# A fused attention and mixture-of-experts kernel: the block lists finished before the second sequence's norm, their constant rows made in the first stage, and the second group of table rows queued behind the first masked scores

## The chip, the cores and the metric

The kernel runs on one core of a Trainium2 chip. The metric is the device time of one execution in microseconds (us). Several executions are timed and their median is given; one further execution is recorded by the profiler. The engines are named as in the profile: PE (matrix multiply), PEld (its weight loads), DVE (vector), ACT (scalar), POOL (GpSimd) and SP (the queue that issues most DMAs). "L586" is line 586 of the kernel.

## The reference

The input x has 8 sequences of 512 tokens of 512 floats. Each token is layer-normed to xn. Two branches use xn:

```
q, k, v = xn@Wq, xn@Wk, xn@Wv              # 16 heads of 32; silu and rotation on q, k
o       = decayed causal linear attention, in chunks of 128 tokens, state carried
s       = (rmsnorm per head of (o * sigmoid(xn@Wg1@Wg2)) * norm_weight) @ Wo
p       = softmax(xn @ gate_w.T);  top 4 of 16 experts, weights renormalised
mixed   = sum over the 4 experts of weight * (silu(xn@Wg[e]) * (xn@Wu[e])) @ Wd[e]
g       = silu(mixed + shared expert * sigmoid(xn @ shared_gate_w))
out     = x + s * g
```

## The kernel before, in words

All arithmetic on PE is in 32-bit floats. The work goes through four stages.

**First stage** (until about 214 us). `first()` norms and transposes each sequence, routes its tokens, and computes the shared expert; sequence 0's attention (`sequence(0, ...)`) is woven in. `sort()` (L375) then ranks all 16,384 token-expert choices: for each choice its row in the list of blocks, `posi` (L459), split into a position and a block number in `sp` (L465). Everything of this stage lies in a pool `p1` on the right side of the on-chip memory, which is closed at L1056.

**Second stage** (about 214 to 301 us). The pool `exps` takes the same memory; its tile `wexp` will hold all 16 experts' weights. Eleven are loaded at once (L1063). The space of the last five (`LATE`) first holds scratch for `table()` (L483), which inverts `posi` into `slot`, the list of the token in each row of each block of 128 rows. For each of 8 groups of 16 choice lists, `make` (L520) writes two tables of zeros and ones on DVE, called `place` and `block`, by comparing `sp` with a row of counts (`count`, an iota at L512); `number` (L538) scales half of `place` by token numbers on ACT; 16 small matmuls `pn` (L566) multiply them, and DVE adds the result into `acc` (L575). The last step multiplies `acc` by `fold` (`pslot`, L582) and writes `slot` (L586). Two homes in `wexp` are used in turn, so group n+2 waits for the `pn` of group n. `table()` is a generator with 33 steps after its first; sequence 1's attention (L1071) calls one step after each of its large matmuls in `product` and `value` (`between[0]`, L618 and L662). Twenty-eight steps are taken in the loop over head groups, four in `value(2, 3)`, and the last one after the sequence (L1072). Steps 30, 31 and 32 are, for the last group, the issue of three expert loads, the 16 matmuls and the addition.

After its loop over the four head groups `sequence(1, ...)` ends with the branch at L869: the gate projection of sequence 2 (`gate_1`), the squares of the norm (`squares`, L777), the reciprocal of the root (`inverse`), the last value product of sequence 2, and `normed` (L794), which broadcasts the scales through PE into the four `a` banks of PSUM and multiplies on DVE (L806).

**Third stage** (about 301 to 706 us). The 136 blocks of 128 gathered tokens are run through their experts: 112 in pairs, then single blocks. For each pair: `gather` (L1110, an indirect DMA issued by POOL), `turn_rows` (L1117, a DMA that transposes, issued by SP), `transpose_x` (L1122, PE), `join` (L1132, copies by ACT: L1138 from PSUM and L1142 from the transposed rows), `prepare` (L1155, DVE copies of one expert's weights, with a run-time offset into `wexp`, and of the row weights), `gate_up` (L1167, PE), and `down` (L1207, PE, again with a run-time offset into `wexp`). Before that come three gathers, `experts_of_blocks` (L1250: six dependent DVE operations giving each block's expert), the four output projections of sequence 1 (`project`, L809, whose results `spill` copies on ACT and stores), and `begin` (L1218), which also does the second half of sequence 2's gate (`gate_2`). The last two experts are loaded from ACT's DMA queue (L1077).

**Fourth stage** (about 706 us to the end): sequences 2 to 7's attention, the gathers of each token's four expert results and the output.

Order of work: the framework derives all waits from the tiles read and written, and it orders each engine's queue by its own schedule. The kernel overrides that order in places. `on_pe()` chains most matmuls of the attention in the order in which they are traced. `behind(engine)` (L216) and `tc.issue_after(ins)` put an instruction behind another one in the same engine's queue, without a wait for its end. Tiles with one `tag` share `bufs` places. With `reuse_waits="tile"` the tiles of a pool wait for the tiles that held the memory before.

The lines that set the order around the change:

```python
        if n == FIRST:
            gate_1(n)
            squares(b)
            inverse(b)
            value(n, 3)
            normed(b)
            return
...
    sequence(1, lambda: None, spill)
    for _ in filling:
        pass
...
    for j in range(3):
        gather(j)
    experts_of_blocks()
    for t in range(NC):
        spill(FIRST - 1, t, project(FIRST - 1, t))
```

Of the kernel before, what the change touches and what calls it, by code (L numbers as in the profile page):

```python
# [19 lines left out]
P = 128  # L20
# [17 lines left out]
TMP = 4  # L38
# [59 lines left out]
def tile_block(ctx: ExitStack, tc: tile.TileContext, a: dict, out: bass.AP):  # L98
# [93 lines left out]
    posi = p1.tile([P, TOPK, NT], I32, tag="posi", name="posi")  # L192

    sp = const.tile([P, 2, TOPK * NT], F16, tag="slot", name="sp")

    eoff = const.tile([P, 2, NBQ], I32, tag="eoff", name="eoff")
# [286 lines left out]
    def table(room):  # L483
# [16 lines left out]
        count = part(2 * NB, QUAD)  # L500
# [7 lines left out]
        half_token, fold, acc = flat(NT), flat(HALF), flat(2 * NB)  # L508
        nc.scalar.copy(half_token, token)
        for h in range(0, P, HALF):  # L510
            nc.scalar.copy(fold[h : h + HALF], ident[h : h + HALF, h : h + HALF])
        nc.gpsimd.iota(  # L512
            count, [[1, 2 * NB], [0, QUAD]], base=0, channel_multiplier=0,
            allow_small_or_imprecise_dtypes=True)
# [5 lines left out]
        def make(i):  # L520
            place, block = homes[i // GROUP % 2]
            for u in range(0, quads, quads // 2):
# [6 lines left out]
                nc.vector.tensor_tensor(  # L529
                    place[:, us], counts(HALF), rows(sp[:, 0, lists], HALF), ALU.is_equal)  # L530
                if u == 0:
# [3 lines left out]
                nc.vector.tensor_tensor(  # L535
                    block[:, us], counts(2 * NB), rows(sp[:, 1, lists], 2 * NB), ALU.is_equal)
# [49 lines left out]
        nc.vector.tensor_scalar(t, pt[:, :NB], float(B * N // 2), None, ALU.add)  # L586
# [113 lines left out]

    def scores(b, g):
# [44 lines left out]
        for j in range(HG):  # L746
            s = scr[0].tile([P, NC, C], F32, tag="sc", name=f"sc_{b}_{g}_{j}", bufs=4)
            nc.vector.tensor_tensor(  # L748
                s, pss[j].rearrange("p (c t) -> p c t", t=C),
                dmask[:, g * HG + j].unsqueeze(1).to_broadcast([P, NC, C]), ALU.mult)  # L750
            sc_of[g].append(s)
# [41 lines left out]

    def normed(b):  # L794
# [9 lines left out]
        for c in range(NC):  # L804
            oc = on_of[b][:, :, c * C : (c + 1) * C]
            nc.vector.tensor_tensor(  # L806
                oc, oc, pbs[c].rearrange("p (g t) -> p g t", t=C), ALU.mult)
# [10 lines left out]
    def enter(b, step=lambda: None, ps=None):  # L818
# [9 lines left out]
        step()  # L828

    def sequence(b, step, projected, before=None, defer=False, also=lambda: None):  # L830
# [197 lines left out]
    halves(0)  # L1028
    xs_of.pop(0)
# [58 lines left out]
    homes = [blkp.tile([P, ROW], U16, tag=f"xg{j}", name=f"xg{j}") for j in range(HOMES // 2)]  # L1088
    homes += [more[:, j * ROW : (j + 1) * ROW] for j in range(HOMES // 2)]
# [11 lines left out]
    by_dve = [0]  # L1101

# [7 lines left out]
    def gather(j, its):  # L1110
        for i in its:
            nc.gpsimd.indirect_dma_start(  # L1112
                out=row(i), out_offset=None, in_=xn_d,
                in_offset=bass.IndirectOffsetOnAxis(ap=slot[:, i : i + 1], axis=0))
# [17 lines left out]
    def join(j, its):  # L1132
# [8 lines left out]
        for u in range(n):  # L1141
            (nc.vector.tensor_copy if j in by_dve else nc.scalar.copy)(  # L1142
                xt[:, u, KP:, :].bitcast(U16).rearrange("p k (t h) -> p h k t", h=2),
                pls[j % 2][:, u].rearrange("p (h k) t -> p h k t", h=2))
# [99 lines left out]
    def aside(j):  # L1244
        if j == PAIRS:
# [4 lines left out]
    def experts_of_blocks():  # L1250
        half = NBQ * 2 * E
        room = xts.rearrange("p j u k t -> p (j u k t)")
        cm = room[:, :half].rearrange("p (b e) -> p b e", e=2 * E)
        ef = room[:, half : half + NBQ]
        ei = room[:, half + NBQ : half + 2 * NBQ].bitcast(I32)
        nc.vector.tensor_tensor(
# [206 lines left out]
```

## Time and profile before

| | |
|---|---|
| median of 3 runs | 1152.28 us (1148.9 to 1152.95) |
| the profiled execution | 1155.04 us |
| its span, from the first to the last instruction | 1153.2 us |
| busy in the span: PE, DVE, ACT, POOL | 1117.9, 736.7, 429.3, 446.8 us |
| mean granted TensorE clock | 0.99 |
| instructions | 21330 |

How to read it: the profile lists instructions by engine and time, and ahead of an instruction the idle time of its engine with what ended it. A matmul's share of "busy" is not a share of its peak. The span is what the instructions cover; the profiled execution took 1.84 us more than that. The waits of PE before 330 us are listed in the answer on PE's waits; the stretch from 225 to 330 us is the one that the change touches, and outside it PE is busy almost throughout.

### The profile page before, as it was taken

The page shows a single profiled execution, that of the slowest core. Times are in us where ns is not written, and L with a number is a line of the kernel's source. Part 1 is how long each engine was busy: PE and PEld are TensorE (multiplying, and loading weights), DVE is VectorE, ACT ScalarE, POOL GpSimd, SP SyncE. Part 2 cuts the span into 40 slices and gives each one's busy share as a digit, 9 for nine tenths or more (in the row PEclk, how much of TensorE's full clock was granted, in tenths as well). Part 3 has the DMA queues.
Part 4 walks back from the last instruction along what each step waited for, and adds up shares of the span by engine and source line. Part 5 has one row for each costly group of instructions (what it writes and reads, how often), then busy time and mean ns, then how long its engine had stood idle before and what let it go on. Part 6 is the DMA issues. An engine that isn't in the chain of part 4 may idle for free. (4 is left out here: it accounts for less than half of the span.)

```text
span 1153.2 us, 21330 instructions
## 1 busy us (share of the span) xinstructions
PE 1117.9 (97%) x7670; PEld 679.7 (59%) x7670; DVE 736.7 (64%) x1580; ACT 429.3 (37%) x927; POOL 446.8 (39%) x427
## 2 busy tenths in 40 slices
PE   7999999989899999999999999999999999999998
PEld 4445554445477777777777775555645545545554
DVE  6358734899334444555444445968879597697784
ACT  3223424154253333333333342353351522522541
POOL 3213100300233333333333322764877857958211
PEclk9999999989999999999999999999999999999999
DMA  9975431191799999999999994833737637434012
GB/s 338 319 276 194 156 127 47 51 352 40 217 200 236 220 244 238 238 241 237 253 233 234 272 215 178 323 101 108 254 116 230 183 108 244 150 122 145 29 36 75
DMA packets 163931, 218.49 MB, mean 189 GB/s; under 512 B 89840, under 2 KB 99184, under 8 KB 161776
## 3 DMA queue, kind: packets, MB, share of 16 engines
q1 hardware_dynamic: 142416, 145.18, 40.5%
q0 software_dynamic: 21120, 70.34, 23.9%
q10 hardware_dynamic: 288, 1.57, 0.4%
q8 instruction: 63, 1.03, 0.4%
q14 instruction: 44, 0.36, 0.1%
HBM read 126.78 MB, written 72.43 MB: 173 GB/s over the span
## 5 line engine op out<-in xcount | busy, mean ns | idle before, releaser
L1180 PE MATMUL pgu<-xts,wst 128*128 128x256 f32 x896 | 204.3, 381 | 0.0
L1180 PEld LDWEIGHTS pgu<-xts,wst 128*128 128x128 f32 x896 | 171.3, 191 | 46.7 <-issue 13.4
L1112 POOL DMA_INDIRECT xg<-xn_d,slot x69 | 65.7, 953 | 229.4 <-DVE w L1163 118.4
L1313 POOL DMA_INDIRECT yg<-y_d,place x128 | 142.5, 1113 | 31.1 <-issue 18.5
L1215 DVE TENSOR_SCALAR y<-py,w 128x512 f32<-128x512 f32 x136 | 101.6, 750 | 44.7 <-PE py L1211 31.0
L1211 PE MATMUL py<-wexp,slb 128*128 x272 | 129.9, 593 | 0.0
L615 PE MATMUL pv<-wv,xT 128*128 128x512 f32 x256 | 120.1, 610 | 3.1 <-DMA xT<-xT_d 2.0
L659 PE MATMUL pq<-xT,wq 128*128 128x512 f32 x256 | 118.2, 604 | 0.3 <-PEq L1278 0.3
L659 PE MATMUL pk<-xT,wk 128*128 128x512 f32 x256 | 118.2, 603 | 0.0
L1192 ACT ACTIVATE slb<-pgu 128x256 f32<-128x256 f32 (+1 forms) x80 | 28.1, 351 | 222.5 <-PE pgu L1180 184.1
L813 PE MATMUL pw<-wo,on 128*128 128x512 f32 x224 | 103.9, 612 | 5.8 <-DVE m L1351 5.8
L1193 DVE TENSOR_TENSOR slb<-slb,pgu 128x256 f32<-128x256 f32 (+1 forms) x80 | 30.5, 381 | 119.5 <-ACT slb L1192 118.1
L1112 POOL DMA_INDIRECT more<-xn_d,slot x67 | 63.5, 948 | 93.1 <-DVE w L1163 56.9
L1355 POOL TENSOR_TENSOR xo<-xo,m 128x512 f32<-128x512 f32 x31 | 45.3, 1460 | 131.2 <-DVE m L1351 123.3
L1142 ACT COPY xts<-pl 128x512 uint16<-128x512 uint16 x110 | 84.1, 767 | 9.0 <-DMA pl<-xg 9.0
L659 PEld LDWEIGHTS pq<-xT,wq 128*128 128x128 f32 x256 | 48.1, 193 | 55.3 <-issue 53.9
L748 DVE TENSOR_TENSOR sc<-ps,dmask 128x512 f32<-128x512 f32 x128 | 79.0, 676 | 0.9 <-PE ps L723 0.9
L615 PEld LDWEIGHTS pv<-wv,xT 128*128 128x128 f32 x256 | 46.3, 191 | 53.7 <-issue 47.1
L813 PEld LDWEIGHTS pw<-wo,on 128*128 128x128 f32 x224 | 42.5, 196 | 57.1 <-issue 47.7
L659 PEld LDWEIGHTS pk<-xT,wk 128*128 128x128 f32 x256 | 46.2, 189 | 50.7 <-issue 48.3
L1161 DVE COPY wst<-wexp 128x512 f32 x112 | 42.8, 424 | 39.8 <-DVE y L1215 18.7
L1211 PEld LDWEIGHTS py<-wexp,slb 128*128 128x128 f32 x272 | 45.5, 191 | 27.4 <-issue 26.8
(196 smaller groups left out, 1716.5 us busy)
## 6 DMA issues: line engine op xcount, KB each, us to landing
y_d<-y SPq DMA_DIRECT2D x136, 256.0 KB
wexp<-in_experts SPq DMA_DIRECT2D x14, 768.0 KB
sh_d<-sh SPq DMA_DIRECT2D x32, 256.0 KB
xT<-xT_d SPq DMA_DIRECT2D x8, 1024.0 KB
m<-sh_d SPq DMA_DIRECT2D x32, 256.0 KB
xo<-in_x SPq DMA_DIRECT2D x32, 256.0 KB
out<-xo SPq DMA_DIRECT2D x31, 256.0 KB
x<-in_x SPq DMA_DIRECT2D x7, 1024.0 KB
```

Source lines behind the costliest of these rows:

```text
L615: nc.tensor.matmul(pv, lhsT=xT_of[b][:, k, t * P : (t + 1) * P], rhs=wv[:, k, :], start=(k == 0), stop=(k == KC - 1))
L659: nc.tensor.matmul(ps, lhsT=w[:, k, g * P : (g + 1) * P], rhs=xT_of[b][:, k, :], start=(k == 0), stop=(k == KC - 1))
L748: nc.vector.tensor_tensor(s, pss[j].rearrange("p (c t) -> p c t", t=C), dmask[:, g * HG + j].unsqueeze(1).to_broadcast([P, NC, C]), ALU.mult)
L813: nc.tensor.matmul(pw, lhsT=on_of[b][:, g, t * P : (t + 1) * P], rhs=wo[:, g, :], start=(g == 0), stop=(g == G - 1))
L1112: nc.gpsimd.indirect_dma_start(out=row(i), out_offset=None, in_=xn_d, in_offset=bass.IndirectOffsetOnAxis(ap=slot[:, i : i + 1], axis=0))
L1142: (nc.vector.tensor_copy if j in by_dve else nc.scalar.copy)(xt[:, u, KP:, :].bitcast(U16).rearrange("p k (t h) -> p h k t", h=2), pls[j % ...
L1161: nc.vector.tensor_copy(to, wflat[:, bass.ds(off + u * KC * F, KC * F)])
L1180: nc.tensor.matmul(pg[:, o * 2 * P : (o + 1) * 2 * P], lhsT=wst[j % 2][k // KP][:, (k % KP * 2 + o) * F :][:, :F], rhs=xt[:, :, k, :], sta ...
L1211: nc.tensor.matmul(py, lhsT=hT[:, u * P : (u + 1) * P], rhs=wflat[:, bass.ds(off + KC * 2 * F, D)], start=True, stop=True)
L1215: gone.append(nc.vector.tensor_scalar(y, py, w[:, u : u + 1], None, ALU.mult).ins)
L1313: nc.gpsimd.indirect_dma_start(out=yg, out_offset=None, in_=y_d, in_offset=bass.IndirectOffsetOnAxis(ap=place[:, r, g : g + 1], axis=0))
L1355: nc.gpsimd.tensor_tensor(xo, xo, m, ALU.add)
```

## The change

- `TMP`, the number of places for the tag `tmp` (rotated keys and queries, spilled projections, block results), goes from 4 to 5.
- `count`, `half_token` and `fold` move out of the scratch in `wexp` into tiles of their own, and are made on POOL in the first stage, behind `halves(0)`. `posi` moves from the pool `p1` to `const`.
- In `make`, the two comparisons of the first half of group 1 are queued behind the last masked score of DVE so far (L748).
- In sequence 1, the last five steps of `table()` come right after the loop over head groups: four of them, `gate_1`, and the fifth. `experts_of_blocks` follows `inverse`, with its scratch now in `wexp`, each operation queued behind the last.
- The loads of the last two experts move from ACT's queue, before the blocks, to SP's queue in the block loop at j = 1 and j = 3.
- The block rows' homes swap: the first three gathers now write to the memory of sequence 1's values. Gathers, row transposes, the copies L1142 and the first run-time offsets are tied to the order in which they are traced.

```diff
-TMP = 4
+TMP = 5
...
-    posi = p1.tile([P, TOPK, NT], I32, tag="posi", name="posi")
+    posi = const.tile([P, TOPK, NT], I32, tag="posi", name="posi")
+    count = const.tile([P, 2 * NB, QUAD], F16, tag="count", name="count")
+    half_token = const.tile([P, NT], F16, tag="half_token", name="half_token")
+    fold = const.tile([P, HALF], F16, tag="fold", name="fold")
...
-        count = part(2 * NB, QUAD)
...
-        half_token, fold, acc = flat(NT), flat(HALF), flat(2 * NB)
-        nc.scalar.copy(half_token, token)
-        for h in range(0, P, HALF):
-            nc.scalar.copy(fold[h : h + HALF], ident[h : h + HALF, h : h + HALF])
-        nc.gpsimd.iota(
-            count, [[1, 2 * NB], [0, QUAD]], base=0, channel_multiplier=0,
-            allow_small_or_imprecise_dtypes=True)
+        acc = flat(2 * NB)
...
-                nc.vector.tensor_tensor(
-                    place[:, us], counts(HALF), rows(sp[:, 0, lists], HALF), ALU.is_equal)
+                with tc.issue_after(masked[0]) if i == GROUP and u == 0 else nullcontext():
+                    nc.vector.tensor_tensor(
+                        place[:, us], counts(HALF), rows(sp[:, 0, lists], HALF), ALU.is_equal)
+                with tc.issue_after(masked[0]) if i == GROUP and u == 0 else nullcontext():
+                    nc.vector.tensor_tensor(
+                        block[:, us], counts(2 * NB), rows(sp[:, 1, lists], 2 * NB),
+                        ALU.is_equal)
...
-        nc.vector.tensor_scalar(t, pt[:, :NB], float(B * N // 2), None, ALU.add)
+        with behind(DVE):
+            nc.vector.tensor_scalar(t, pt[:, :NB], float(B * N // 2), None, ALU.add)
...
-            nc.vector.tensor_tensor(
+            masked[:] = [nc.vector.tensor_tensor(
                 s, pss[j].rearrange("p (c t) -> p c t", t=C),
-                dmask[:, g * HG + j].unsqueeze(1).to_broadcast([P, NC, C]), ALU.mult)
+                dmask[:, g * HG + j].unsqueeze(1).to_broadcast([P, NC, C]), ALU.mult).ins]
...
-            nc.vector.tensor_tensor(
-                oc, oc, pbs[c].rearrange("p (g t) -> p g t", t=C), ALU.mult)
+            scaled[:] = [nc.vector.tensor_tensor(
+                oc, oc, pbs[c].rearrange("p (g t) -> p g t", t=C), ALU.mult).ins]
...
+    def experts_of_blocks():
+        half = NBQ * 2 * E
+        room = wflat[:, (E - LATE // 2) * WE :]
...
+        with behind(DVE):
+            nc.vector.tensor_reduce(ef, cm, axis=AX.X, op=ALU.add)
...
         if n == FIRST:
+            for _ in range(4):
+                next(filling)
             gate_1(n)
+            next(filling, None)
             squares(b)
             inverse(b)
+            experts_of_blocks()
             value(n, 3)
             normed(b)
             return
...
     halves(0)
+    with behind(POOL):
+        nc.gpsimd.tensor_copy(half_token, token)
+    for h in range(0, P, HALF):
+        with behind(POOL):
+            nc.gpsimd.tensor_copy(fold[h : h + HALF], ident[h : h + HALF, h : h + HALF])
+    with behind(POOL):
+        nc.gpsimd.iota(
+            count, [[1, 2 * NB], [0, QUAD]], base=0, channel_multiplier=0,
+            allow_small_or_imprecise_dtypes=True)
...
-    for _ in filling:
-        pass
     between[0] = lambda: None
     slot = slots[0]
-    for e in range(E - LATE // 2, E):
-        nc.scalar.dma_start(wexp[:, e, :], a["experts"][:, e, :])
     left.close()
...
-    homes = [blkp.tile([P, ROW], U16, tag=f"xg{j}", name=f"xg{j}") for j in range(HOMES // 2)]
-    homes += [more[:, j * ROW : (j + 1) * ROW] for j in range(HOMES // 2)]
+    homes = [more[:, j * ROW : (j + 1) * ROW] for j in range(HOMES // 2)]
+    homes += [blkp.tile([P, ROW], U16, tag=f"xg{j}", name=f"xg{j}") for j in range(HOMES // 2)]
...
         for u, i in enumerate(its):
-            nc.sync.dma_start_transpose(pls[j % 2][:, u], row(i)[:, D : 2 * D])
+            with tc.issue_after(turned[-1]) if turned else nullcontext():
+                turned.append(nc.sync.dma_start_transpose(
+                    pls[j % 2][:, u], row(i)[:, D : 2 * D]).ins)
...
-            (nc.vector.tensor_copy if j in by_dve else nc.scalar.copy)(
-                xt[:, u, KP:, :].bitcast(U16).rearrange("p k (t h) -> p h k t", h=2),
-                pls[j % 2][:, u].rearrange("p (h k) t -> p h k t", h=2))
+            with behind(DVE if j in by_dve else ACT):
+                (nc.vector.tensor_copy if j in by_dve else nc.scalar.copy)(
+                    xt[:, u, KP:, :].bitcast(U16).rearrange("p k (t h) -> p h k t", h=2),
+                    pls[j % 2][:, u].rearrange("p (h k) t -> p h k t", h=2))
...
     def aside(j):
+        if j in (1, 3):
+            e = E - LATE // 2 + j // 2
+            nc.sync.dma_start(wexp[:, e, :], a["experts"][:, e, :])
         if j == PAIRS:
             load_xT(FIRST)
...
     for j in range(3):
         gather(j)
-    experts_of_blocks()
     for t in range(NC):
         spill(FIRST - 1, t, project(FIRST - 1, t))
     on_of.pop(FIRST - 1)
+    gone += scaled
     begin(0, lambda: gate_2(FIRST, banks="aakd"))
```

The gathers (L1112) are also put `behind(POOL)`, and `turned` is cleared in the branch for more than 136 blocks.

More of the change, by code (lines that the diff above doesn't have):

```diff
@@ L534, in make @@
                             :, : GROUP // 2], HALF), ALU.mult)
-                nc.vector.tensor_tensor(
-                    block[:, us], counts(2 * NB), rows(sp[:, 1, lists], 2 * NB), ALU.is_equal)
         def number(i, some):
@@ L699, in by_token @@
         kd_of[g] = pk[:, (NC - 1) * P :], kd
+    masked = []
     def scores(b, g):
@@ L792, in inverse @@
         nc.vector.reciprocal(rs_of[b], rs_of[b])
+    scaled = []
     def normed(b):
@@ L805, in normed @@
             oc = on_of[b][:, :, c * C : (c + 1) * C]
-            nc.vector.tensor_tensor(
-                oc, oc, pbs[c].rearrange("p (g t) -> p g t", t=C), ALU.mult)
+            scaled[:] = [nc.vector.tensor_tensor(
+                oc, oc, pbs[c].rearrange("p (g t) -> p g t", t=C), ALU.mult).ins]
     def project(b, t):
@@ L828, in enter @@
         step()
+    def experts_of_blocks():
+        half = NBQ * 2 * E
+        room = wflat[:, (E - LATE // 2) * WE :]
+        cm = room[:, :half].rearrange("p (b e) -> p b e", e=2 * E)
+        ef = room[:, half : half + NBQ]
+        ei = room[:, half + NBQ : half + 2 * NBQ].bitcast(I32)
+        with behind(DVE):
+            nc.vector.tensor_tensor(
+                cm, end.rearrange("p w e -> p (w e)").unsqueeze(1).to_broadcast([P, NBQ, 2 * E]),
+                iota_b.unsqueeze(2).to_broadcast([P, NBQ, 2 * E]), ALU.is_le)
+        with behind(DVE):
+            nc.vector.tensor_reduce(ef, cm, axis=AX.X, op=ALU.add)
+        with behind(DVE):
+            nc.vector.tensor_copy(ei, ef)
+        with behind(DVE):
+            nc.vector.tensor_scalar(ei, ei, E - 1, None, ALU.bitwise_and)
+        with behind(DVE):
+            nc.vector.tensor_scalar(eoff[:, 0], ei, float(WE), None, ALU.mult)
+        with behind(DVE):
+            nc.vector.tensor_scalar(eoff[:, 1], ei, float(D), None, ALU.add)
     def sequence(b, step, projected, before=None, defer=False, also=lambda: None):
@@ L1101, in tile_block @@
     by_dve = [0]
+    turned = []
     def inside(f):
@@ L1111, in gather @@
         for i in its:
-            nc.gpsimd.indirect_dma_start(
-                out=row(i), out_offset=None, in_=xn_d,
-                in_offset=bass.IndirectOffsetOnAxis(ap=slot[:, i : i + 1], axis=0))
+            with behind(POOL):
+                nc.gpsimd.indirect_dma_start(
+                    out=row(i), out_offset=None, in_=xn_d,
+                    in_offset=bass.IndirectOffsetOnAxis(ap=slot[:, i : i + 1], axis=0))
     @inside
@@ L1248, in tile_block @@
     kept.clear()
[L1250 to L1256, printed above, removed]
-            cm, end.rearrange("p w e -> p (w e)").unsqueeze(1).to_broadcast([P, NBQ, 2 * E]),
-            iota_b.unsqueeze(2).to_broadcast([P, NBQ, 2 * E]), ALU.is_le)
-        nc.vector.tensor_reduce(ef, cm, axis=AX.X, op=ALU.add)
-        nc.vector.tensor_copy(ei, ef)
-        nc.vector.tensor_scalar(ei, ei, E - 1, None, ALU.bitwise_and)
-        nc.vector.tensor_scalar(eoff[:, 0], ei, float(WE), None, ALU.mult)
-        nc.vector.tensor_scalar(eoff[:, 1], ei, float(D), None, ALU.add)
     for j in range(3):
         gather(j)
-    experts_of_blocks()
     for t in range(NC):
@@ L1281, in tile_block @@
         gone.clear()
+        turned.clear()
         for j in range(3):
```

## The prediction

> **What bounds the kernel now.** I read the page first (PE is busy 97% of the span), then PE's waits, then the timelines of PE, DVE, ACT and POOL from 225 to 330 us. After 330 us PE is busy without a break until the blocks end, so only the transition into the blocks can give time. PE's idle time there, with the rows after it:
>
> ```profile
> 237.35 0.90 PE L691 MATMUL pk<-ident,kT 128*128 128x128 f32 x3 [4.16 <-DVE state L738]
> 238.04 5.19 PE L659 MATMUL pq<-xT,wq 128*128 128x512 f32 x6
> ...
> 255.87 2.74 PE L659 MATMUL pq<-xT,wq 128*128 128x512 f32 x6
> ...
> 265.92 4.54 PE L615 MATMUL pv<-wv,xT 128*128 128x512 f32 x6 [2.02 <-DMA xT<-xT_d]
> ...
> 300.83 0.26 PE L582 MATMUL pslot<-wexp 128*64 128x143 f16 x2 [2.76 <-DVE on L806]
> 301.01 15.67 PE L813 MATMUL pw<-wo,on 128*128 128x512 f32 x32
> ...
> 319.88 1.15 PE L645 MATMUL p<-g,wg 32*128 32x128 f32 x26 [1.90 <-ACT so L996]
> 320.97 5.41 PE L1180 MATMUL pgu<-xts,wst 128*128 128x256 f32 x16
> 326.21 0.60 PE L1126 MATMUL pt<-ident,more 128*128 128x128 f32 x4
> 326.65 3.62 PE L1180 MATMUL pgu<-xts,wst 128*128 128x256 f32 x16
> ```
>
> The reader sees four idle times, and that what follows each runs slowly: six matmuls of pq took 5.19 us after the first and 2.74 us undisturbed; 16 of pgu took 5.41 and then 3.62. The granted clock in the 5 us after them is 0.61 to 0.69, elsewhere 1.00. So each idle time is paid almost twice. DVE in the same stretch:
>
> ```profile
> 224.77 0.29 DVE L465 CAST sp<-bl 128x256 f16<-128x256 int32 x1
> 229.48 0.43 DVE L529 TENSOR_TENSOR wexp<-wexp,sp 128x512 f16<-128x512 f16 x1 [4.42 <-POOL wexp L512]
> ...
> 236.54 0.18 DVE L736 COPY state<-pk 128x32 f32<-128x32 f32 x1
> ...
> 297.00 1.36 DVE L1256 TENSOR_TENSOR xts<-end,iota_b 128x1152 f32<-128x1152 f32 x1 [0.60 <-PE pv L615]
> ...
> 300.09 2.47 DVE L806 TENSOR_TENSOR on<-on,pb 128x512 f32<-128x512 f32 x4
> 302.48 0.30 DVE L586 TENSOR_SCALAR slot<-pslot 128x143 int32<-128x143 f32 x1
> ...
> 305.13 0.76 DVE L1161 COPY wst<-wexp 128x512 f32 x2 [2.17 <-DMA wexp<-in_experts]
> ```
>
> `sp` is ready at 225.06, but the tables start only at 229.48: DVE waits for POOL's iota, and POOL waited for the store of posi, which holds the memory of `wexp`. Then two groups of tables (7.1 us) stand ahead of the state copies at 236.54, for which PE's transposes wait. Later L1256 and its five followers stand ahead of L806, and `slot` comes last.
>
> ```profile
> 226.21 3.24 POOL L512 IOTA wexp<- 128x572 f16 x1 [9.01 <-DMA at_d<-posi]
> ...
> 303.68 1.23 POOL L1112 DMA_INDIRECT xg<-xn_d,slot  x1 [71.49 <-DVE eoff L1263]
> ```
>
> ```profile
> 318.01 1.38 ACT L1142 COPY xts<-pl 128x512 uint16<-128x512 uint16 x2 [7.53 <-DMA pl<-xg]
> 319.26 1.05 ACT L996 COPY so<-pw 128x512 f32<-128x512 f32 x2
> ```
>
> The gather starts at 303.68; its transposed rows reach ACT at 318.01. ACT stands in wait for them with two spill copies queued behind, and those hold the PSUM bank for which PE waits at 317.99. That chain (slot, gather, transposed rows, spill, gate, first pgu) sets when the blocks begin.
>
> **Part A, 225 to 289 us: −6.5 us.** The iota and the copies leave the path, and posi no longer holds `wexp`, so the first tables can start at 225.06: 4.42 us earlier. DVE is nearly full: from 229.48 to 288.15 it is busy 55.68 of 58.67 us, so it can gain at most 4.42 + 2.99 = 7.4 us. The second group is put behind the masked scores, whose matmuls end at 229.5, so the state copies run at about 229.3 instead of 236.54 and the transposes need not wait. PE then saves 4.16 us idle, 5.19 − 2.74 = 2.45 of slow pq, and 0.90 − 0.49 = 0.41 of slow transposes (0.49 is the next such group): 7.0 us. The 2.02 us before pv stays: that load of xT is issued when the last pq has read the old xT, so it moves along with PE. What becomes late next is DVE, at 4.4 to 7.4 us. I take 6.5, nearer to PE's 7.0 since both bounds lie close; the range keeps 4.4 to 7.4.
>
> **Part B, 289 us to the end of the first pgu: −7.3 us.** The last `pn` and `pslot` go ahead of the squares, so `slot` needs: output ends at 289.13, pn 1.2 us, the addition 0.45, fold 0.26, L586 0.30: about 292 against 302.8 us. Gather and transposed rows took 303.68 to 318.01 = 14.3 us; from 293 they end at about 308 (310 if the three expert loads issued at 287.4 slow them), before the projections end at about 312. So ACT no longer stands in front of the spill copies, and the 1.90 us goes, with the slow pgu, 5.41 − 3.62 = 1.79. The six expert operations (3.4 us by 297.00 to 300.1 and 302.7 to 302.95, less the slot between them) now start after the reciprocal, which in this alignment ends at about 294.3, so they end at 297.8; the broadcast on PE ends at about 297.4, and the first L806 then takes 0.6. PE waits about 1.1 instead of 2.76 us. An idle time of 1.04 us earlier in this trace left the clock at full, so I also count the slow projections away: 15.67 − 14.00 (the same 32 matmuls at 214.12) = 1.67. With the 0.25 before the last square: 1.66 + 0.25 + 1.67 + 1.90 + 1.79 = 7.3 us. If the rows came late after all, 3.7 of it would be lost.
>
> A rule may be weighed here. The Trainium skill, "TensorE: Matmul & The Clock Gate", section "HAM oscillation — how this bites in real kernels", says that idle times above some 3.4 us are what throttles the array. This trace disagrees: 1.90, 2.02 and 2.76 us were each followed by slow matmuls, though 1.91 us at 1025.87 was not. By the rule the 1.67 and 1.79 would not be gained, and the total would be 3.5 us less.
>
> **Part C, the two late expert loads: +3 us.** DVE's L1161 and PE's L1211 read `wexp` at run-time offsets. The row at 305.13 shows that the very first such read waits for the last expert's load, so a read waits for all loads traced before it. At j = 1 the load is issued after the weight copies of pair 2, which end about 0.7 us after the first pgu; the first `down` follows that pgu by 4.3 us (326.21 to 330.54). The load of one expert took 301.12 to 305.13 = 4.0 us at a DMA share of 0.75; in the blocks the share is about 1.0. So PE would stand 0.4 us if it lands in 4.0, and 4.4 us in 8. At j = 3 the copies leave 5.3 us by the same spacing: 0 to 2.7 us. A slow clock adds up to 1.7 each. The schedule may also put the next pgu in front, and then nothing is lost. Bounds 0 and 10 us; I take 3, nearest to landing in 5 to 6 us.
>
> **What costs nothing.** The three copies and the iota in the first stage take at most 3 × 0.71 (a POOL copy of 128x512) + 3.24 = 5.4 us and fit into POOL's idle time before 25.03:
>
> ```profile
> 16.34 2.85 POOL L268 COPY hs<-x 128x512 uint16<-128x512 uint16 x4
> 25.03 0.24 POOL L251 TENSOR_SCALAR rstd<-mv 128x4 f32<-128x4 f32 x1 [5.83 <-DVE mx L328]
> ```
>
> Without that cover rstd would be late, but DVE has 4.94 us idle at 34.69 behind it. A rule speaks against this move: the Trainium skill, "GPSIMD Engine Reference", section "Key points", says that POOL shares its SBUF interfaces with DVE and contends with two-input DVE work. No row shows the iota beside DVE work. By the rule DVE could lose up to the iota's length there, and the idle time just named would still take it.
>
> The fifth `tmp` place, the order of gathers, row transposes and L1142 change no duration. In the blocks PE is never idle, so they can cost only if they hold PE up; ACT needs about 2.5 of each 5.6 us per pair. In the last stage the fifth place can shift DVE's order; the idle times there (1.16, 2.61, 1.91) bound that at about 2 us either way, and I take 0. SP loses nothing: today it waits 5.6 us for spill copies behind ACT's L543 at 232, and that goes with the earlier tables.
>
> **Sum.** −6.5 − 7.3 + 3 = −10.8 us. Against the profiled execution (1155.04, span 1153.2, so 1.84 around it) that is 1144.2. That execution lies 2.76 us above the median of the runs, so against the median 1152.28 I forecast 1141.5 us.
>
> **Rivals.**
> 1. *DVE becomes the bound of part A.* It is already 95% busy there; if the moved group only pushes other table work in front of PE, A gives 2 to 4 us instead of 6.5: 1144 to 1146, say 1145.5. For: tables, rotations and masks fill DVE from 244 to 285. Against: its own chain starts 4.42 us earlier. Chance 0.13.
> 2. *The earlier slot buys nothing*, because the gathers or the transposed rows wait for something else (the memory of the first stage's tiles, the three expert loads at 287 us). Then B gives only 1.91 of the first gap and the square's 0.25: −6.5 − 1.9 + 3 = −5.4: 1147. Against: values of sequence 1 are last read at 289.13, before `slot`. Chance 0.09. This is also the case in which the change does not do what it says.
> 3. *Slower: the late loads stall the blocks.* Each run-time read waits for a load that competes with a saturated DMA. A and B give 13.8 us, so it decides once the two loads take more than about 11.5 us each: (11.5 − 3.7) + (11.5 − 5.3) = 14; at 14 us each PE loses 19, and with two slow spells 22: 1160. For: the DMA share of about 1. Against: 4.0 us in the one row. Chance 0.06.
>
> **How the numbers follow.** Forecast 0.72: from A 5 to 7.4, B 6 to 7.3, C 0 to 6, that is 1138 to 1146, likeliest 1141.5. The range takes in C at 0 with 2 us from the last stage, and rivals 1 and 2: 1135.5 to 1148.5. A measurement here tells apart about 0.5%, or 5.8 us: below 1146.5 counts as faster. The forecast and most of rival 1 lie below: 0.84; rival 2 and the rest within: 0.10; slower 0.06.
>
> **What would show it.** Right: the first L529 starts at about 225; no wait of PE for L738; L586 at about 285 and the first gather one us later; no wait of ACT's L1142 ahead of L996; the first pgu at about 307 to 308 and taking 3.6 us; the L512 iota before 25 us. Part C is seen in a wait of PE L1211 or DVE L1161 for wexp's loads between 310 and 330 us. Wrong would be: new waits of PE for DVE between 240 and 283, a first pgu after 312, or PE idle in the blocks for more than 6 us.

## The result, and the profile after

The changed kernel is slower: 1158.7 us median of 5 runs (1157.96 to 1163.64), beside 1152.65 us (1148.9 to 1153.13) for the kernel before. The ratio is 1.0068, with a 95% interval of 1.0041 to 1.0095. The profiled execution took 1163.64 us with a span of 1161.8 us, at the same mean clock of 0.99. It is the longest of the five; a second profile of the same kernel (`after_again` below: 1159.73 us, span 1157.9) lies closer to the median, so the table gives both.

Stages are cut where PE starts or ends named matmuls: "ps" is the first score of sequence 1, "pq" its last query product, "pv" its first value product of the group that needs the new xT. "pw" are the output projections, "pgu" and "py" the gate-and-up and the down products of the blocks. The column `best4` is a kernel described further below. Times in us.

| stretch | before | after | after_again | best4 |
|---|---|---|---|---|
| start to first pw | 214.1 | 217.2 | 213.8 | 214.0 |
| to first ps | 14.3 | 14.3 | 14.2 | 14.3 |
| to end of last pq | 32.4 | 27.8 | 27.8 | 26.3 |
| to pv (waits for xT) | 5.1 | 7.1 | 6.8 | 5.4 |
| to end of last output of sequence 1 | 23.2 | 24.1 | 22.9 | 23.2 |
| to projections' first pw | 11.9 | 9.4 | 9.4 | 9.1 |
| to first pgu of the blocks | 20.0 | 16.1 | 16.2 | 16.1 |
| first pgu | 5.2 | 3.5 | 3.5 | 3.5 |
| rest of the pairs | 308.5 | 322.6 | 322.5 | 308.5 |
| single blocks | 75.1 | 79.0 | 80.0 | 75.7 |
| rest | 443.3 | 440.7 | 440.7 | 439.7 |

PE's timeline of the changed kernel (columns: start, length, engine, line, operation, out<-in, shape, count; in brackets the idle time before and what ended it):

```profile
243.40 1.31 PE L645 MATMUL p<-g,wg 32*128 32x128 f32 x24 [1.38 <-DVE wexp L576]
244.64 1.50 PE L766 MATMUL po<-qd,state 32*32 32x128 f32 x24
246.08 1.83 PE L772 MATMUL po<-sc,v 128*32 128x128 f32 x32
...
266.36 5.42 PE L615 MATMUL pv<-wv,xT 128*128 128x512 f32 x6 [3.95 <-DMA xT<-xT_d]
...
299.88 14.00 PE L817 MATMUL pw<-wo,on 128*128 128x512 f32 x32 [1.34 <-DVE on L810]
316.00 3.69 PE L1219 MATMUL pgu<-xts,wst 128*128 128x256 f32 x16
```

The 4.16 us wait for the state copies is gone, and so are the slow projections (14.00 instead of 15.67) and the wait and slow clock at the first pgu. But the wait for xT grew from 2.02 to 3.95 us, and a wait of 1.38 us is new. DVE and POOL of the same kernel:

```profile
227.89 0.29 DVE L468 CAST sp<-bl 128x256 f16<-128x256 int32 x1
228.64 0.42 DVE L526 TENSOR_TENSOR wexp<-count,sp 128x512 f16<-128x512 f16 x1 [0.46 <-DVE sp L468]
...
233.77 0.18 DVE L738 COPY state<-pk 128x32 f32<-128x32 f32 x1
...
292.83 0.31 DVE L586 TENSOR_SCALAR slot<-pslot 128x143 int32<-128x143 f32 x1 [0.74 <-PE pslot L581]
294.69 0.95 DVE L794 RECIPROCAL rs<-rs 128x128 f32<-128x128 f32 x1 [1.55 <-ACT rs L790]
295.56 1.29 DVE L841 TENSOR_TENSOR wexp<-end,iota_b 128x1152 f32<-128x1152 f32 x1
```

```profile
20.97 3.24 POOL L1064 IOTA count<- 128x572 f16 x1
...
28.11 0.23 POOL L254 TENSOR_SCALAR rstd<-mv 128x4 f32<-128x4 f32 x1 [3.91 <-DVE mx L331]
...
293.44 1.23 POOL L1148 DMA_INDIRECT more<-xn_d,slot  x1 [69.14 <-PE pr L786]
```

The tables start 0.46 us after `sp` instead of 4.42; `slot` is written ahead of the reciprocal; the gather follows at 293.44; the iota lies hidden, with 3.91 us of POOL's idle time still behind it. What is lost lies in the blocks. PE there, and then SP:

```profile
323.42 0.60 PE L1164 MATMUL pt<-ident,more 128*128 128x128 f32 x4
328.36 3.75 PE L1250 MATMUL py<-wexp,slb 128*128 x4 [4.35 <-DMA wexp<-in_experts]
331.91 4.17 PE L1219 MATMUL pgu<-xts,wst 128*128 128x256 f32 x16
...
336.35 1.88 PE L1250 MATMUL py<-wexp,slb 128*128 x4
...
341.96 1.89 PE L1219 MATMUL pgu<-xts,wst 128*128 128x256 f32 x8
348.11 3.78 PE L1250 MATMUL py<-wexp,slb 128*128 x4 [4.26 <-DMA wexp<-in_experts]
351.69 2.79 PE L1219 MATMUL pgu<-xts,wst 128*128 128x256 f32 x8
```

```profile
317.97 3.25 SPq L1156 DMA_TRANSPOSE pl<-more  x2
321.32 0.53 SPq L1286 DMA_DIRECT2D wexp<-in_experts  x1
...
338.34 2.56 SPq L1156 DMA_TRANSPOSE pl<-more  x2
340.95 1.06 SPq L1255 DMA_DIRECT2D y_d<-y  x2
342.12 0.38 SPq L1286 DMA_DIRECT2D wexp<-in_experts  x1
```

Each load (L1286) is followed by one wait of `down` (L1250) for it. The first is issued at 321.32 and awaited until 328.36, which is 7.0 us; the second from 342.12 to 348.11, 6.0 us. After each the clock is low: py takes 3.75 and 3.78 instead of 1.88, 16 pgu 4.17 instead of 3.62, 8 of them 2.79 instead of 1.89. The granted clock was 0.58 from 328 to 334 us. Together: 4.35 + 4.26 + 1.87 + 1.90 + 0.55 + 0.90 = 13.8 of the 14.1 us that the pairs lost. In the single blocks PE waits four times for copies that it had not waited for; the first and the longest:

```profile
652.33 1.13 PE L1225 MATMUL pgu<-wexp,xt 128*128 x4 [0.57 <-ACT xt L1181]
...
677.58 1.13 PE L1225 MATMUL pgu<-wexp,xt 128*128 x4 [0.96 <-ACT xt L1181]
```

### The profile page after: what moved, and what is told of

Read it like the earlier page. It is cut to its first block, busy times and chain, and to the rows that moved or that the text cites. A ratio compares the mean times of both kernels' runs of the same rounds, so it can differ in the third digit from the quotient of the medians.

```text
span 1161.8 us, 21323 instructions
## 1 busy us (share of the span) xinstructions
PE 1120.9 (96%) x7670; PEld 679.9 (59%) x7670; DVE 738.9 (64%) x1580; ACT 434.7 (37%) x924; POOL 447.6 (39%) x430
## 5 line engine op out<-in xcount | busy, mean ns | idle before, releaser
L1148 POOL DMA_INDIRECT more<-xn_d,slot x69 | 66.0, 956 | 243.4 <-DVE w L1202 86.2
L1250 PE MATMUL py<-wexp,slb 128*128 x272 | 133.8, 608 | 8.6 <-DMA wexp<-in_experts 8.6
L659 PE MATMUL pq<-xT,wq 128*128 128x512 f32 x256 | 115.7, 593 | 0.3 <-PEq L1305 0.3
L817 PE MATMUL pw<-wo,on 128*128 128x512 f32 x224 | 100.6, 596 | 5.7 <-DVE m L1379 4.4
L1148 POOL DMA_INDIRECT xg<-xn_d,slot x67 | 63.3, 945 | 99.0 <-DVE w L1202 57.0
L1181 ACT COPY xts<-pl 128x512 uint16<-128x512 uint16 x110 | 76.6, 767 | 0.0
L1250 PEld LDWEIGHTS py<-wexp,slb 128*128 128x128 f32 x272 | 46.5, 195 | 37.7 <-issue 32.9
```

Of the source, the lines that this page charges most:

```text
L659: nc.tensor.matmul(ps, lhsT=w[:, k, g * P : (g + 1) * P], rhs=xT_of[b][:, k, :], start=(k == 0), stop=(k == KC - 1))
L817: nc.tensor.matmul(pw, lhsT=on_of[b][:, g, t * P : (t + 1) * P], rhs=wo[:, g, :], start=(g == 0), stop=(g == G - 1))
L1148: nc.gpsimd.indirect_dma_start(out=row(i), out_offset=None, in_=xn_d, in_offset=bass.IndirectOffsetOnAxis(ap=slot[:, i : i + 1], axis=0))
L1181: (nc.vector.tensor_copy if j in by_dve else nc.scalar.copy)(xt[:, u, KP:, :].bitcast(U16).rearrange("p k (t h) -> p h k t", h=2), pls[j % ...
L1250: nc.tensor.matmul(py, lhsT=hT[:, u * P : (u + 1) * P], rhs=wflat[:, bass.ds(off + KC * 2 * F, D)], start=True, stop=True)
```

## The experiments

The theory after the result: the loss lies in the pairs, because a read of `wexp` at a run-time offset declares the whole tile, so that each late load first waits for earlier reads and then holds up later ones (`down` is such a read); the single blocks lose by the copies' pinned place, and sequence 1 by xT's load. The rivals stand in the expectations.

One condition for reading the numbers: the first four runs, and the last two, were on a chip on which the kernel before took 1163.43 and 1162.3 us, with gaps on PE in the last stage that no wait explains; the last stage of the changed kernels takes about 450 us there and 440 elsewhere, and the pairs without a stall 309.8 to 310.2 instead of 308.5. Each ratio is to the kernel before on the same chip (1152.1 to 1152.3 us for the other eight).

### Where the late loads stand

`loads_before_blocks`: the loads go back to ACT's queue.

```diff
     slot = slots[0]
+    for e in range(E - LATE // 2, E):
+        nc.scalar.dma_start(wexp[:, e, :], a["experts"][:, e, :])
...
-        if j in (1, 3):
-            e = E - LATE // 2 + j // 2
-            nc.sync.dma_start(wexp[:, e, :], a["experts"][:, e, :])
```

> The changed kernel with one part undone: the loads of the last two experts are issued again from ACT's queue before the blocks. Theory (the late loads stall PE because every run-time read of the expert weights traced after them waits for them): both waits of PE L1250 for these loads (4.35 and 4.26 us in the changed kernel) and the slow matmuls behind them go, 14 us in all, so about 1158.7 - 14 = 1145 us, unless the early loads delay the first gathers; that would show as a first pgu later than 316 us and cost up to 4 us. Rival (the loads as such crowd the DMA queues of the block stage, wherever they stand): less than 5 us is gained, 1154 us or more.

Measured: 1165.03 us, ratio 1.001 (0.9988 to 1.0032). The pairs take 310.2 us and the waits for the loads are gone, but part B lost most of its gain: with `slot` so early, the issue now stands ahead of the norm's root on ACT. ACT's timeline of this kernel:

```profile
290.36 2.87 ACTq L1113 DMA_DIRECT2D wexp<-in_experts  x1
293.27 1.28 ACT L790 ACT_TABLE_LOAD   x1 [3.00 <-issue]
294.56 0.37 ACT L790 ACTIVATE rs<-pr,eps_rms 128x128 f32<-128x128 f32 x1
```

PE then waits 1.34 us for the reciprocal and 2.91 us for L810, and the projections are slow again. So the forecast 1145 us was missed, but the loads do cost the pairs their time, and ACT's queue is no longer a free place for them.

`narrow_reads`: the loads stay, and the reads of the first eight pairs declare a range that ends before the two experts. It holds only because the blocks are sorted by expert and these pairs belong to earlier experts.

```diff
-            off = on_dve(0, its[0], 0, (E - 1) * WE)
+            off = on_dve(0, its[0], 0, (E - 1 if j >= 8 else E - 3) * WE)
...
-                max_val=(E - 1) * WE, bass_reorder=False,
+                max_val=(E - 1 if j >= 8 else E - 3) * WE, bass_reorder=False,
```

> The changed kernel, with the two late loads where they are, but the declared range of the run-time offset of pairs 0 to 7 ends before the last two experts (the first pairs belong to the first experts, so the same weights are read). Theory (the stall is a wait on the declared range of the read and not a lack of data or of DMA time): PE no longer waits at L1250, 14 us go, about 1145 us. Rival (the stall comes from the DMA traffic of the load, which delays gathers and transposed rows as well): PE then waits for other things in the same place and less than 5 us is gained.

Measured: 1160.85 us, ratio 0.9971 (0.9954 to 0.9988): faster than the kernel before, with the loads still written in the block loop. No L1250 wait is left, the pairs take 310.2 us, and SP issues the loads at 291.67 and 303.45, ahead of the first pgu at 315.35, as they need not wait for the first pairs' reads. So the stall comes from the declared range. Since both loads run before the blocks in this kernel, it does not part the two sides of that range: the late issue, and the later reads' wait for it. PE's waits also show that xT's load now stands out:

```profile
PE pv L615 <- DMA xT<-xT_d: 7.7, 1, 7.7
```

(in total, times, longest, in us.)

`before_late_loads`: the kernel before, with this one part of the change.

```diff
-    for e in range(E - LATE // 2, E):
-        nc.scalar.dma_start(wexp[:, e, :], a["experts"][:, e, :])
...
+        if j in (1, 3):
+            e = E - LATE // 2 + j // 2
+            nc.sync.dma_start(wexp[:, e, :], a["experts"][:, e, :])
```

> The kernel before with one part of the change alone: the loads of the last two experts are issued on SP in the block loop at j = 1 and j = 3. Theory: the two stalls of about 7 us each appear here as well, less some 2 us for the wait of DVE L1161 for the load that is now late, so 1152.6 + 10 to 14 = 1163 to 1167 us, with two waits of PE for wexp's loads. Rival (the stalls belong to the new order of rows and gathers): about 1152 us.

Measured: 1175.07 us, ratio 1.0107 (1.0076 to 1.0138). The pairs take 318.4 us, 9.9 more than the profile of the kernel before, of which up to 1.7 may belong to the chip. One wait for the loads came and not the two expected (at the place of the first, PE waits 0.90 us for DVE). PE's waits:

```profile
PE py L1209 <- DMA wexp<-in_experts: 6.4, 1, 6.4
```

The part alone makes the kernel slower by 1.1%, with none of the others present.

`sync_loads`: the changed kernel, with the two loads issued once on SP where `loads_before_blocks` has them on ACT (`nc.sync` for `nc.scalar`).

> The changed kernel, with the two late expert loads issued once by SyncE right after the slots instead of inside the blocks. Theory (the blocks lose about 14 us because the load first waits for earlier reads of the declared range and the later reads wait for the load): pair blocks 308 to 311 us instead of 322.5, ScalarE not held up by an issue, first gate as in after; single blocks still 79 to 80; 11 to 14 us below after, ratio to the kernel before 0.994 to 0.998. Rival (on SyncE the loads now stand ahead of the row transposes, so the rows come late and ScalarE stands in front of the spill copies again): the 1.9 us wait before the first gate and a slow first pgu are back, 3.7 us lost, ratio about 0.999.

Measured: 1147.71 us, ratio 0.9963 (0.9944 to 0.9981). The pairs take 308.5 us, the stretch to the first pgu 15.9. PE's timeline at the place of the first stall:

```profile
315.87 3.64 PE L1221 MATMUL pgu<-xts,wst 128*128 128x256 f32 x16
319.35 0.60 PE L1166 MATMUL pt<-ident,more 128*128 128x128 f32 x4
319.79 1.88 PE L1252 MATMUL py<-wexp,slb 128*128 x4
321.51 3.62 PE L1221 MATMUL pgu<-xts,wst 128*128 128x256 f32 x16
```

py follows its transposes without a bracket. The rival's late rows did not come. This moves two DMA issues alone and turns the change from 0.7% slower into 0.4% faster: 12 us below the median of `after_again`, 1159.73.

### The copies in the single blocks

`free_join`: the copies L1181 are not queued behind ACT's last instruction.

```diff
-            with behind(DVE if j in by_dve else ACT):
+            with behind(DVE) if j in by_dve else nullcontext():
```

> The changed kernel, with ACT's copies of the transposed rows (L1181) no longer queued behind the copy from PSUM (L1176). Theory (queueing them puts the copies late in the stage of single blocks, where PE waits 2.7 us for them and loses 3.8 us in all): those waits go there, but the copies again stand ahead of two spill copies before the blocks, which costs up to 1.9 + 1.8 us there; so 1155 to 1158.7 us, with no wait of PE for L1181 after 640 us. Rival (the waits after 640 us come from the transposed rows landing late, by their chained issue on SP): PE still waits there, and the time is 1158 us or more.

Measured: 1167.15 us, ratio 1.0036 (1.002 to 1.0053). The single blocks are back at 75.1 us (the loads still stall). ACT's rows show why: in the changed kernel ACT stands up to 3.91 us for transposed rows in the stretch from 645 to 665 us, with later work queued behind; here at most 1.15. But the pin also did good. Without it ACT again stands before the blocks in wait for transposed rows, with two spill copies behind, although the gathers run early:

```profile
304.60 1.38 ACT L1181 COPY xts<-pl 128x512 uint16<-128x512 uint16 x2 [10.72 <-DMA pl<-more]
305.85 1.05 ACT L1025 COPY so<-pw 128x512 f32<-128x512 f32 x2
```

and PE waits for those copies:

```profile
306.47 7.13 PE L817 MATMUL pw<-wo,on 128*128 128x512 f32 x16 [3.17 <-ACT so L1025]
```

This costs 3.4 us in the stretch to the first pgu (19.6 us, and 16.2 in `narrow_reads` on the same chip). So the pin should hold in the pairs only (`if n == 2 else nullcontext()`), as in `mended`, `best3` and `best4`, where both stretches are short.

### The yardstick, xT's load and the masked scores

`after_again`: no edit.

> The changed kernel unaltered, as the yardstick of the three kernels beside it. Both theories: the ratio to the kernel before inside or close to the first comparison's interval (1.0041 to 1.0095). If the 3.1 us that the first profiled execution lost at the start (block gates' first matmul 5.91 instead of 3.70 us) belong to that execution alone, the stretch up to the first pw is 213 to 215 us here; if they belong to the change, 217.

Measured: 1159.73 us, ratio 1.0068 (1.0038 to 1.0098). The first stretch is 213.8 us, so the 3.1 us belonged to one profiled execution.

`xT_first`: the three expert loads of `table()` (L555) are queued behind xT's load. Expert 13's comes first of them, early in sequence 1, since `count` no longer lies in its space.

```diff
-                for e in range(E - LATE, E - LATE // 2):
-                    nc.sync.dma_start(wexp[:, e, :], a["experts"][:, e, :])
+                with tc.issue_after(xT_ins[0]):
+                    for e in range(E - LATE, E - LATE // 2):
+                        nc.sync.dma_start(wexp[:, e, :], a["experts"][:, e, :])
```

> The changed kernel with expert 13 and its neighbour's early loads queued behind xT's load. Theory (those 768 KB compete with xT): the stretch from the end of the last pq to the first pv is 5 to 5.5 us instead of 7.1, and the first pv is 4.5 instead of 5.4 us; 2 to 3 us below after_again. Rival (xT's load is slow because the earlier row gathers and transposes stand in its way): 7 us as before, no difference in time.

Measured: 1159.09 us, ratio 1.0054 (1.0032 to 1.0075): no difference. PE waits for xT no shorter than before:

```profile
263.63 4.83 PE L618 MATMUL pv<-wv,xT 128*128 128x512 f32 x6 [5.37 <-DMA xT<-xT_d]
```

In this profile my theory of a competing expert load fell. It is not settled by it: `mended` below holds the same edit, also with the zero stores ahead, and there xT came in 5.1 us from its issue (255.40 to 260.54), against 7.6 here. SP's queue of the changed kernel says what else stands ahead:

```profile
243.61 12.29 SPq L1105 DMA_DIRECT2D y_d<-none  x7
257.41 0.33 SPq L555 DMA_DIRECT2D wexp<-in_experts  x1
259.35 0.32 SPq L597 DMA_DIRECT2D xT<-xT_d  x1
```

Seven stores of zeros, issued until 255.90, behind eleven expert loads. In the kernel before they ended at 255.47 and xT's load was issued 5.4 us later; now it is 3.5 us later. Between the two the DMA share was 0.54 before, and 1.07 in the changed kernel: the DMA engines were still fully busy when xT was asked for. `stores_behind` moves the stores too:

```diff
-    for i in range(SURE, NB):
-        nc.sync.dma_start(y_d[i * P : (i + 1) * P, :], none)
...
+                    for i2 in range(SURE, NB):
+                        nc.sync.dma_start(y_d[i2 * P : (i2 + 1) * P, :], none)
```

(added inside the `issue_after` of `xT_first`; `none` gets a tile of its own.)

> The changed kernel with xT's load ahead of expert 13's early load and ahead of the seven zero stores (256 KB each) that it has stood behind. Theory (xT's load is as slow as the transfers queued ahead of it; with TensorE 4 to 7 us earlier it meets their backlog): 5.0 to 5.5 us from the end of the last pq to the first pv instead of 7 to 8.4, first pv 4.5 instead of 5.4 us, about 2.5 us below after, ratio to the kernel before 1.003 to 1.006. Rival (the expert loads themselves are the backlog): 7 us stay, no difference.

Measured: 1156.13 us, ratio 1.0036 (1.0015 to 1.0057). xT's load comes in 5.0 us and pv runs at 4.54 again:

```profile
254.84 0.33 SPq L602 DMA_DIRECT2D xT<-xT_d  x1
255.21 0.43 SPq L556 DMA_DIRECT2D wexp<-in_experts  x1
255.69 4.39 SPq L558 DMA_DIRECT2D y_d<-none  x7
```

```profile
259.79 4.54 PE L620 MATMUL pv<-wv,xT 128*128 128x512 f32 x6 [1.89 <-DMA xT<-xT_d]
```

From the first ps to the end of sequence 1's outputs it takes 26.3 + 5.0 + 23.2 = 54.5 us, 6.2 less than before; in the changed kernel 57.5 to 59.0. The 26.3 instead of 27.8 is not the stores' doing: `xT_first` and `sync_loads` have it too, because the po matmuls after the 1.4 us wait ran at full clock there. The 5.0 comes with both expert load and stores moved, so the share of each is open; over all kernels with the change xT took 5.0 to 5.6 us from issue to pv with both behind it, and 6.8 to 9.4 with one or both ahead, but for `mended`.

`unmasked`: the second group's first rows do not wait for the masked scores (`if True:` in place of both `issue_after(masked[0])`).

> The changed kernel without the wait of the second group's first two table rows for the first masked scores. Theory (this wait is what took away TensorE's 4.16 us wait for the state copies): TensorE waits 3 to 5 us there again, the stretch from the first ps to the end of the last pq is 31 to 33 us instead of 27.8, and the time is 3 to 5 us above after_again. Rival (moving count to the first stage alone did it): the stretch stays at 28 us, no difference.

Measured: 1164.66 us, ratio 1.0114 (1.0092 to 1.0137), but not for the reason expected. DVE works off all 7.1 us of tables first and still reaches the state copies in time, since it starts as early as in `after`. DVE and PE of this kernel:

```profile
225.79 0.42 DVE L526 TENSOR_TENSOR wexp<-count,sp 128x512 f16<-128x512 f16 x1 [0.46 <-DVE sp L468]
...
232.85 0.18 DVE L738 COPY state<-pk 128x32 f32<-128x32 f32 x1
```

```profile
233.66 0.55 PE L691 MATMUL pk<-ident,kT 128*128 128x128 f32 x3 [0.24 <-DVE state L740]
```

The theory failed here: 0.24 us of wait came back, not 3 to 5, and the stretch to the last pq takes 26.3 us. The earlier start of the tables (`count` made in the first stage, `posi` out of the way) had removed the wait; the pin on the masked scores is worth about nothing there. The 3.7 us by which this profile is longer than `after_again` lie mainly elsewhere: 9.3 instead of 6.8 us for xT, 24.0 instead of 22.9 after it, 82.2 instead of 80.0 in the single blocks, less 1.5 in the stretch itself. That xT comes later when PE asks earlier fits the backlog; why the single blocks vary between 77.8 and 82.2 us with the pin in place was not settled.

### All repairs together

`mended`: `narrow_reads`, `xT_first` and the pin in pairs only.

> Three edits on the changed kernel: the first eight pairs of blocks declare a run-time range that ends before the two late experts; the xT copies keep their place behind ScalarE and VectorE only where the block is a pair; expert 13 and its neighbour's early loads wait for xT's load. Theory (the loss lies in the stall on the late experts, in the single blocks' copies and in xT's load): pair blocks 310 us instead of 322, single blocks 75 instead of 79, xT's load landing in 5 to 5.5 us instead of 7.0, so 16 to 19 us below after_again: ratio to the kernel before 0.988 to 0.994. Rival (the stalls cover other work that then becomes the bound): under 8 us below after_again, not below the kernel before.

Measured: 1140.03 us, ratio 0.9904 (0.9881 to 0.9926), 20 us below `after_again`. Pairs 308.5, single blocks 75.6, pv 5.2 us after the last pq.

`best3` holds for any routing: `sync_loads`, `stores_behind`, the pin in pairs only, `unmasked`. `best4` is the same with `narrow_reads` in place of `sync_loads`.

> All repairs that hold for any routing: the late loads once on SyncE, xT's load ahead of expert 13's load and of the zero stores, the xT copies pinned only in pairs, the second group's table rows free of the wait for the masked scores. Theory: the single gains add up, 12 + 4 + 2.5 + 1 us below after, ratio to the kernel before 0.987 to 0.992. Rival (the repairs overlap, or SyncE's order costs the rows): 0.993 to 0.998.

> As best3, but the late loads stay inside the blocks and the first eight pairs declare a range that ends before them. Theory: as the loads start late there and disturb no transposed row, the same as best3 or up to 2 us less, ratio to the kernel before 0.985 to 0.992. Rival: SyncE's order costs more here, 0.993 to 0.998.

Measured: 1139.01 us, ratio 0.9877 (0.9857 to 0.9898), and 1137.51 us, ratio 0.9861 (0.9837 to 0.9885). Both beat both kernels. Their intervals overlap, so which of the two is better is open. The premise that the loads start late in `best4` did not hold: SP issues them at 285.51 and 299.13, in `best3` at 287.00 and 299.75.

### The fifth place for `tmp`

> The kernel best4 unaltered, as the yardstick of the run beside it: ratio to the kernel before 0.984 to 0.989, last stage 439.7 us.

> best4 with four tmp places instead of five. Theory (the fifth place is what shortened TensorE's wait of 2.61 us for m in the last stage, and took the slow pw matmuls behind it away): the 2.6 us wait and a pw group of 5.3 instead of 3.7 us are back, last stage 442 to 443 us instead of 439.7, 2.5 to 3.5 us above best4. Rival (the fifth place changes no duration, as the prediction had it, and another alignment did it): last stage 439.7 us, no difference in time.

`best4_tmp4` sets `TMP` back from 5 to 4. Measured: `best4_again` 1153.16 us, ratio 0.992 (0.9895 to 0.9945), on the slower chip and not the 0.984 to 0.989 expected, so the gain of `best4` is 0.8% there and 1.4% elsewhere; `best4_tmp4` 1154.34 us, ratio 0.9918 (0.9891 to 0.9945). The profiles speak for the theory (last stage 453.5 instead of 450.2 us). PE waits longer for m, and a slow group is there that `best4_again` does not have:

```profile
1022.40 5.40 PE L822 MATMUL pw<-wo,on 128*128 128x512 f32 x8 [1.91 <-DVE m L1382]
```

The other profiles point the same way: with four places the last stage takes 443.3 us (before) against 439.6 to 440.7 in nine profiles with five, and on the slower chip 451.8 and 453.5 against 450.2 to 450.9. In the kernel before, one wait for m is 2.61 us with a pw group of 5.34 behind it, at the same place 1.14 and 3.70 in the changed kernel. But the timed runs show no difference, and 3 us is about the width of their interval. So it is not shown that the fifth place shortened the last stage by 2.6 us.

## Why the prediction was wrong

**Part C failed: 14 us instead of 3.** The form of the sum was right: `down` came due 4.3 us after the first pgu (324.02 less 319.69), where 4.3 was said, and the copies ended 0.47 us after it, where 0.7 was said. Three sizes were wrong. First, the slack: the load did not start when the copies ended, for SP had two row transposes in front of it, and at j = 3 two stores of results as well (issue 1.16 and 2.2 us after the copies). The second `down` also came due 3.9 us after its copies, not 5.3. That left 2.7 us until `down` at the first and 1.7 at the second, not 3.7 and 5.3. Second, I took landing in 5 to 6 us; it was 7.0 and 6.0. Third, the slow clock, 2.4 and 2.8 us, was put only in the bounds, at 1.7 each. With the measured terms: (7.0 − 2.7) + (6.0 − 1.7) + 5.2 = 13.8. The size varies: in the profiles of `stores_behind` and `xT_first`, with the same two loads, the pairs take 319.9 and 325.6 us, 11 and 17 more than before. The upper bound of 10 allowed 8 us for a load, more than was measured, and was too low by the slack and the slow clock. The same two waits of PE, 8.6 us together, are the sign of being wrong that the forecast named (PE idle in the blocks for more than 6 us).

**Rival 3 was the right mechanism with the wrong point.** It was to decide when both loads take more than 11.5 us. With the slack and the slow clock as measured, two loads of 6.6 us each already cost 14 us: 2 × 6.6 − 4.4 + 5.2.

**Part A: 1.7 to 3.2 us instead of 6.5.** The tables, the state copies and the missing wait came as forecast. One step that failed is "that load of xT ... moves along with PE". Its issue moved 5.0 us earlier and its landing only 3.3 (255.81 to 262.61 in `after_again`, 260.85 to 265.92 before): it met busy DMA engines, and 1.7 to 2.0 us of the gain went there. With expert load and zero stores moved behind it, part A gives 6.2 us, of which 1.5 is the clock. The other step is a new wait of PE for DVE, which the forecast had named as a sign against it: 1.3 to 1.4 us (L576, DVE's copy of the first `pn`), with slow po matmuls behind it that cost another 1.5. The reason given for the early state copies was also too much: they needed the earlier tables, not the pin on the masked scores. So the first pgu came at 311.1 us in `after_again`, where 307 to 308 was said.

**Part B: 8.1 us, forecast 7.3, in part by luck.** Order and the two slow groups came as worked out; the 1.34 us wait ahead of the projections was forecast as 1.1 and left the clock at full. But the reason given for the 3.7 us at the spill copies (rows by 308, before the projections end) does not hold by itself: in `free_join` the rows reached ACT at 304.60 and two spill copies still stood behind them, which cost 3.4 us. The gain came with the pin on L1142, to which the forecast gave nothing. Rival 2 is out: the gathers did follow the slot.

**"Change no duration" was wrong for L1142.** PE being busy throughout the pairs does not say that the single blocks can bear the pin. It cost 3.9 to 4.9 us there, and `free_join` shows that it is the pin; ahead of the blocks it gave 3.4. For the fifth `tmp` place the forecast of 0 stands beside a gain of 2.6 us in the last stage whose cause is not shown.

**The sum.** In the spans of `after_again` and before: −3.2 − 8.0 + 14.0 + 4.9 − 2.6, and −0.4 in the first two stretches, is +4.7 us. The medians lie 6.1 and 7.5 us apart, as the profiled execution of the kernel before, 1155.04 us, was longer than its five timed runs. Without the stalls and the pin's cost `after_again` would stand at 1159.73 − 14.0 − 4.9 = 1140.8 us, and `mended` takes 1140.03. That is the forecast number, 1141.5, but not its sum: the 2.6 us of the last stage, forecast as 0, make up for most of what part A fell short.

**Readings.** Three figures of the forecast do not come out again; the sum does not rest on them. The clock over 5 us from each of the four matmuls behind a wait reads 0.50, 0.66, 0.66 and 0.66, not 0.61 to 0.69. The DMA share during the load of 4.0 us reads 0.67, not 0.75. And in rival 2 the 1.91 us already holds the square's 0.25.

## What to carry to other kernels

When a load is moved into a loop that reads the same tile at run-time offsets, ask for both sides of the declared range: which earlier reads hold back its issue, and which later reads hold for its landing. Time it from its place in the issuing queue, with everything in front of it, and add the slow clock behind each stall. When PE is made to ask for a transfer earlier, look what the DMA queues still hold at that moment: part of the gain can end there. And when a gain comes as forecast, ask which of the edits made it: here a pin that was said to change nothing carried 3.4 us of it.

## What the runs showed of the hardware that was not expected

- The same idle time of PE at the same place was followed by slow matmuls in one kernel and not in another. PE's timelines of `mended` and of `sync_loads` at one step:

```profile
239.49 1.15 PE L648 MATMUL p<-g,wg 32*128 32x128 f32 x24 [1.36 <-DVE wexp L577]
240.57 1.24 PE L769 MATMUL po<-qd,state 32*32 32x128 f32 x24
241.74 1.93 PE L775 MATMUL po<-sc,v 128*32 128x128 f32 x32
```

```profile
240.44 1.15 PE L645 MATMUL p<-g,wg 32*128 32x128 f32 x24 [1.36 <-DVE wexp L576]
241.52 0.86 PE L766 MATMUL po<-qd,state 32*32 32x128 f32 x24
242.31 1.08 PE L772 MATMUL po<-sc,v 128*32 128x128 f32 x32
```

Both waited 1.36 us; the po matmuls then took 1.24 and 1.93 us in the one, 0.86 and 1.08 in the other. Over the 5 us from that matmul in the changed kernel, after 1.38 us idle, the granted clock was 0.66; in `mended` it was 0.66 as well, and in `sync_loads` from 239 to 244 us 1.00. The Trainium skill, "TensorE: Matmul & The Clock Gate", section "HAM oscillation — how this bites in real kernels", puts the limit at idle times of about 3.4 us; the runs show slow spells well below it, and that the idle time before a matmul alone does not decide.
- Issuing one DMA took ACT 2.87 us at 290.36 in `loads_before_blocks`, and 0.34 us for the second at 299.58. SP took 0.33 us to issue the same load at 288.91 in `sync_loads`. An issue on a computing engine's queue can so cost more than most of its instructions; why the first was so long is open.
- The two 768 KB loads took 7.0 and 6.0 us from issue to the first use in the blocks, though such a load before the blocks had taken 4.0 in the kernel before.
